# A two-layer graph network on one core: two of the last batch's twelve attention units by TensorE's sums and ScalarE's functions, with 18 steps kept for the last change of layers

## The chip, the cores and the metric

The kernel runs on one core of one Trainium2 chip. A core has TensorE (PE; its weight loads are listed apart as PEld), VectorE (DVE), ScalarE (ACT), GpSimd (POOL) and SyncE (SP), which here only issues transfers. The metric is the time of one execution in microseconds of device time. The kernel before took 3831.26 us, the median of three runs from 3830.42 to 3833.37. The profiled execution took 3836.74 us by that clock and its span in the profile is 3835.0 us, so times read from the trace are within 0.2% of the timed ones.

## The reference

The input has 8 batches of 2048 nodes with 256 features, and a symmetric 0/1 matrix `adj`. Two layers follow one another, each with a residual and a normalisation:

```python
# layer 0: chunked attention, softmax within every 256 keys, masked by adj
scores = clip(q k^T / 8, -10, 10);  scores = where(mask == 0, -10, scores)
attn   = softmax(scores, axis=-1)          # within a chunk; chunks are summed
out    = layernorm(attn v Wo^T + bo + x);  x = layernorm(x + out)
# layer 1: graph attention, 4 heads of 64 features
Wh = x @ W;  s_src, s_dst = per-head dot products of Wh with a
e  = s_src[i] + s_dst[j];  e = where(e > 0, e, 0.2 * e)
e  = where(adj != 0, e, -inf);  alpha = softmax over j
h  = elu(alpha @ Wh);           x = layernorm(x + h)
```

## The kernel before

**Layer 0** runs in 64 slots a batch (4 query groups of 512 nodes, 2 head pairs, 8 chunks). A slot s holds on TensorE the scores of slot s+1 (L377), then the two products of slot s (L412), one for each head of the pair. VectorE clips and masks the scores out of PSUM (L388), ScalarE takes the exponential in two halves (`exps`, L400) and copies each product out of PSUM (L419, tile `raw`), VectorE inverts the denominators (L427), GpSimd scales and adds (L434, L436).

**Layer 1** works on *units*: 12 units are the 4 heads times three groups of 6, 5 and 5 node blocks (`BANKS`). A unit has 16 tiles, one for each block of 128 neighbours. A tile is made by `make`: VectorE computes `e = max(srow, gd) * et` with one instruction over 768 or 640 columns (L712), where `srow` holds factors of the source nodes broadcast to all partitions, `gd` one factor a partition, and `et` the 0/1 edges. Then `use` multiplies it on TensorE with the features `waug` (L732) into the PSUM tile `pa`, 24 or 20 small matmuls a tile. After 16 tiles `close` yields in four pieces: denominators `dn` on VectorE (L755, L756), `hh` on ScalarE (L760), `ee` and `hp` on ScalarE (L764, L766), and `h` on VectorE (L768). `rest` takes one such piece at a time. Tiles `e` have 4 buffers.

**How they are interleaved.** All engines take their instructions in the order in which the program writes them. While batch b runs layer 0, each slot also takes one `step` of batch b-1's layer 1: 3 tiles (`STEP`), written between the slot's two products. In the last batch the final `LATE` = 14 slots take no step; these 14 steps (42 tiles) are kept and laid between the pieces of the last *change of layers* (L996 to L999), the stretch in which the last query group's projection, normalisations and layer-1 factors are made and in which no slot runs. Its last pieces are `factors`: `most` and `spread` find the maximum and the exponentials, and `rows` writes the source factors to `rowD` in DRAM and has GpSimd scale `waug` by `ed` in four multiplications (L657, L659). Then `Layer1` for the last batch is created, whose constructor issues its first transfers of `et` and `srow`, and a *last stage* runs its 12 units alone, 64 steps of 3 tiles, with the closing normalisations of batches 6 and 7 (`Close`, tables `CLOSING_ALONE` and `ENDING`) between them. After the last tile come the last `close` and the last two groups' normalisation and output.

**PSUM.** Eight banks: `psA` holds two tiles of two banks (scores and others), `psC` one bank for products, `psL` two banks for `pa`, and `psM` one bank, shared by many small users: the feature product `pw` of one node block (L566), half of the output projection `po` (L523), and the helpers of `factors`. A tile of a pool with one buffer can't be written before the readers of the one before it are done. From the second batch on both products of a slot use `psC`, so the second waits for the copy of the first.

In the last 18 slots of the last batch (46 to 63), `psM` is used behind the slot's second product by `pw` in slots 46 to 49, 62 and 63, and by `po` in slots 51 and 52.

Of the kernel before, what the change touches and what calls it, by code (L numbers as in the profile page):

```python
# [8 lines left out]
F32 = mybir.dt.float32  # L9
# [13 lines left out]
def adj_resnorm_kernel(  # L23
# [42 lines left out]
    FIRST = [sum(BANKS[:m]) for m in range(len(BANKS))]  # L66
    TILES = len(UNITS) * NT
    STEP = TILES // SLOTS
    LATE = 14
    WIDE = max(BANKS)  # L70
    JG = 4
    assert TILES == STEP * SLOTS and NT % JG == 0

# [39 lines left out]
    clipD = [tc.dram_tile([P, NT, CH], I8, name=f"clipD{q}") for q in range(NCH)]  # L113
    edgeD = [tc.dram_tile([P, NT, n * P], U8, name=f"edgeD{m}") for m, n in enumerate(BANKS)]
    rowD = tc.dram_tile([B, H, N], F32, name="rowD")
    x1D = tc.dram_tile([B, N, F], F32, name="x1D")
    ctxD = tc.dram_tile([B, N, F], F32, name="ctxD")

# [283 lines left out]
    def product(s, k, alone):  # L402
        q, hp, c = where[s]
        if k == 0:
            raws[s] = small.tile([P, 2, QT, D1], F32, tag="raw", name="raw")

        pool, tag = (psL, "psL") if alone and k else (psC, "psC")
        pc = pool.tile([P, QT, D1], F32, tag=tag, name="pc")
        for i in range(QT):
            for u in range(KT):  # L410
                for z in range(2):
                    nc.tensor.matmul(  # L412
                        pc[z * D : (z + 1) * D, i, :],
                        lhsT=probs[s][u][:, k, i * P + z * D : i * P + (z + 1) * D],
                        rhs=vaug[:, KT * c + u, 2 * hp + k, :],
                        start=(u == 0),
                        stop=(u == KT - 1),
                    )
        nc.scalar.copy(raws[s][:, k], pc)  # L419
# [191 lines left out]
    AFTER_0 = {i: lambda o, i=i: o.values((i + 1,)) for i in range(3)}  # L611
    AFTER = {0: lambda o: o.values((2,)), 1: lambda o: o.values((3,))}

    def factors(b, sd, waug):

# [14 lines left out]
        def spread():  # L632
            pb = psM.tile([P, CH], F32, tag="psM", name="pb")
            nc.tensor.matmul(
                pb[:, :H],
                lhsT=st["most"].to_broadcast([H, P]),
                rhs=identf[:H, :H],
                start=True,
                stop=True,
            )  # L640
            nc.vector.tensor_copy(top, pb[:, :H])
            nc.vector.tensor_add(s, s, topb)
            nc.vector.tensor_scalar(s, s, FAR, None, ALU.min)
            nc.scalar.activation(s, s, AF.Exp, scale=1.0 - SLOPE)
            nc.vector.tensor_sub(d, d, topb)
            nc.vector.tensor_scalar(d, d, -FAR, None, ALU.max)
            nc.scalar.activation(ed, d, AF.Exp)
            nc.scalar.activation(gd, d, AF.Exp, scale=SLOPE - 1.0)

# [16 lines left out]


    class Layer1:
        def __init__(self, b, gd, waug):
            self.b, self.gd, self.waug = b, gd, waug  # L670
            self.made = self.used = 0
            self.rows, self.edge, self.e = {}, {}, {}
            self.tail = []
            self.load_edge(0)
            self.load_edge(1)
            self.load_row(0)

        def load_row(self, n):
            if n < len(UNITS):
                m, h = UNITS[n]  # L680
                srow = small.tile([P, WIDE * P], F32, tag="srow", name="srow")
                i0, w = FIRST[m] * P, BANKS[m] * P
                nc.sync.dma_start(
                    out=srow[:, :w], in_=rowD[self.b, h, i0 : i0 + w].partition_broadcast(P)
                )
                self.rows[n] = srow

        def load_edge(self, k):
            n, jg = k // (NT // JG), k % (NT // JG)
            if n < len(UNITS):  # L690
                m, _ = UNITS[n]
                et = edges.tile([P, JG, WIDE * P], U8, tag="et", name="et")
                w = BANKS[m] * P
                nc.sync.dma_start(
                    out=et[:, :, :w], in_=edgeD[m][:, jg * JG : (jg + 1) * JG, :]
                )
                self.edge[k] = et

        def make(self):

            if self.made == TILES:
                return
            k = self.made
            n, j = k // NT, k % NT
            m, h = UNITS[n]
            if j == NT // 2:
                self.load_row(n + 1)
            if j % JG == 0:
# [11 lines left out]
            self.e[k] = e  # L720
            self.made += 1

        def use(self):
            k = self.used
            n, j = k // NT, k % NT
            m, h = UNITS[n]
            if j == 0:
                self.pa = psL.tile([P, CH], F32, tag="psL", name="pa")
            e = self.e.pop(k)
            for i in range(BANKS[m]):  # L730
                for z in range(2):
# [15 lines left out]
                    self.tail.pop(0)  # L747

        def close(self, u, pa):
            m, h = UNITS[u]  # L750
            n = BANKS[m]
            pav = pa[:, : n * D1].rearrange("p (k d) -> p k d", k=n)

# [20 lines left out]
                op1=ALU.add,  # L774
            )

        def step(self):
            self.rest(1)
            for _ in range(STEP):
                self.make()  # L780
                self.use()

    class Close:

# [41 lines left out]
    for g in range(NCH):  # L826
# [28 lines left out]
        12: [(3, "stats")],  # L855
        13: [(3, "finish")],
    }
    CLOSING_ALONE = {
        -1: [(0, "load"), (1, "load")],
        1: [(0, "add")],  # L860
        2: [(0, "stats"), (1, "add")],
        3: [(1, "stats")],
        4: [(0, "finish"), (2, "load")],
        5: [(1, "finish"), (3, "load")],
        7: [(2, "add")],
        8: [(2, "stats"), (3, "add")],
        9: [(3, "stats")],
        10: [(2, "finish")],
        11: [(3, "finish")],
    }  # L870
    ENDING = {
        25: [(0, "load")],
        28: [(0, "add")],
        29: [(0, "stats")],
        31: [(0, "finish")],
        46: [(1, "load")],
        49: [(1, "add")],
        50: [(1, "stats")],
        52: [(1, "finish")],
        SLOTS - 1: [(2, "load"), (3, "load")],  # L880
        SLOTS: [(2, "add"), (2, "stats"), (3, "add"), (3, "stats"), (2, "finish"), (3, "finish")],
    }
    lower = None
    for b in range(B):
        waug = blocks.tile([P, NT, H, D1], F32, tag="waug", name="waug")
# [15 lines left out]
        for s in range(SLOTS):  # L901
            q, hp, c = where[s]
            i = s % QS
            send()
            if s + 3 < SLOTS:
                load_slab(s + 3)
# [25 lines left out]
                    step(group)  # L932
            elif closing:
                closing.do(s, behind=False)
            product(s, 0, not lower)
            if s + 1 < SLOTS:
                for u in range(KT):
                    exps(s + 1, u)
# [2 lines left out]
                    lower.step()  # L941
            elif masks.left():
                masks.step()
            product(s, 1, not lower)

            if before and i in after:
                after[i](before)
# [9 lines left out]

        send()
        before = group
        gd, fs = factors(b, sd, waug)  # L960
        group = None
        every = tuple(range(QT))

# [29 lines left out]
        else:  # L993
# [2 lines left out]
            order = [begin, lambda: before.values((2, 3)), steps[0], step, ctx, step, steps[1], step]  # L996
            order += [steps[2], step, steps[3], step, steps[4], step, steps[5], step, steps[6], step]
            order += [steps[7], step, steps[8], step, steps[9], step, fs[0], step, fs[1], step, fs[2]]
            order += [step, lambda: lower.rest(4)]  # L999
            assert sum(p is step for p in order) == LATE  # L1000
        for piece in order:
            send()
            piece()
        send()
        lower = Layer1(b, gd, waug)

    closing, ending = Closing(B - 2, CLOSING_ALONE), Closing(B - 1, ENDING)
    closing.do(-1)
    for _ in range(STEP):
        lower.make()  # L1010
    for s in range(SLOTS + 1):
        send()
        if s < SLOTS:
            lower.step()
        else:
            lower.rest(4)
        closing.do(s)
        ending.do(s)
    send()
# [42 lines left out]
```

## Time and profile before

| stage of the trace, us from the start | length | what it is |
|---|---|---|
| to 3474.1 | 3474.1 | seven batches and 46 slots of the last |
| 3474.1 to 3501.2 | 27.1 | slots 46 to 49, with steps of layer 1 and `pw` |
| 3501.2 to 3571.3 | 70.1 | slots 50 to 63, without steps |
| 3571.3 to 3628.0 | 56.7 | last change of layers, with 14 steps |
| 3628.0 to 3817.2 | 189.2 | last stage, 192 tiles alone |
| 3817.2 to 3835.0 | 17.8 | last close, two normalisations, output |

The page gives the busy share of each engine (PE 96%, DVE 84%, ACT 51%, POOL 36%) and the span in 40 slices of 96 us. The timeline lists instructions in order of time; repeated ones are merged with their count, and the bracket gives the idle time of the engine before it and what ended that. "x60" matmuls at L732 are three tiles of 640 columns. The trace lacks a few per cent of the matmul records, so that counts of matmuls are not exact.

### The profile page before, as it was taken

What the parts mean: (1) busy time and instruction counts of PE and PEld (TensorE: products, weight loads), DVE (VectorE), ACT (ScalarE), POOL (GpSimd) and SP (SyncE); (2) the same over time, 40 slices, a digit from 0 to 9 for tenths busy, and PEclk for the clock granted to TensorE, in tenths of its full rate; (3) what the DMA queues carried; (4) which work ended last, traced back from release to release, by engine and by line L of the source; (5) the groups of instructions that cost most, each with busy time, mean ns of one, the idle gap of its engine ahead of it and who ended that gap; (6) DMA issues with size and microseconds to landing.
All of it is one profiled execution on the core that took longest, in us unless ns stands there. A gap on an engine that the chain in (4) does not pass through costs nothing. (4 is left out here: it accounts for less than half of the span.)

```text
span 3835.0 us, 160246 instructions
## 1 busy us (share of the span) xinstructions
PE 3696.8 (96%) x72100; PEld 2752.3 (72%) x72100; DVE 3203.6 (84%) x4810; ACT 1950.1 (51%) x3601; POOL 1385.1 (36%) x1202
## 2 busy tenths in 40 slices
PE   9999999999999999999999999999999999999787
PEld 5656677776777777776777767777677777776676
DVE  5876499986999789995999959998699978998798
ACT  4666345555555555554555545555455555555321
POOL 1445233333433343343433324333343434334310
PEclk9999999999999999999999999999999999999999
DMA  6652333333333433333433334333333433333354
GB/s 161 151 113 65 77 101 99 96 87 112 105 95 102 91 117 101 97 101 87 131 99 92 98 92 134 97 95 88 110 110 94 104 86 118 104 99 86 93 149 123
DMA packets 756545, 398.50 MB, mean 104 GB/s; under 512 B 425744, under 2 KB 721040, under 8 KB 755856
## 3 DMA queue, kind: packets, MB, share of 16 engines
q1 hardware_dynamic: 705856, 354.54, 36.3%
q10 hardware_dynamic: 50000, 33.70, 2.7%
q8 instruction: 564, 9.24, 1.0%
q14 instruction: 125, 1.02, 0.1%
HBM read 331.22 MB, written 56.89 MB: 101 GB/s over the span
## 5 line engine op out<-in xcount | busy, mean ns | idle before, releaser
L388 DVE SCALAR_TENSOR_TENSOR pr<-ps,slab 128x1024 f32<-128x1024 f32 x1024 | 1192.5, 1205 | 215.7 <-PE ps L377 211.4
L712 DVE SCALAR_TENSOR_TENSOR e<-srow,gd,et 128x640 f32<-128x640 f32 (+1 forms) x1536 | 1349.1, 934 | 11.2 <-DMA srow<-rowD 5.7
L412 PEld LDWEIGHTS pc<-vaug,pr 128*64 128x64 f32 x32768 | 1040.6, 138 | 442.7 <-issue 253.7
L412 PE MATMUL pc<-vaug,pr 128*64 128x65 f32 x32768 | 1158.4, 224 | 40.9 <-ACT raw L419 32.0
L400 ACT ACTIVATE pr<-pr 128x1024 f32<-128x1024 f32 x1024 | 1050.4, 1057 | 158.1 <-DVE pr L388 143.6
L732 PE MATMUL pa<-waug,e 128*64 128x65 f32 x32768 | 1083.2, 224 | 41.1 <-DVE e L712 39.6
L732 PEld LDWEIGHTS pa<-waug,e 128*64 128x64 f32 x32768 | 1020.8, 139 | 67.7 <-DVE e L712 39.2
L377 PE MATMUL ps<-qT,kT 64*128 64x512 f32 x4096 | 1029.0, 619 | 3.6 <-DVE pr L388 2.6
L434 POOL TENSOR_TENSOR part<-raw,rd 128x512 f32<-128x512 f32 x448 | 467.9, 1044 | 1462.9 <-DVE rd L427 1450.4
L419 ACT COPY raw<-pc 128x260 f32<-128x260 f32 x1024 | 384.9, 377 | 1181.6 <-PE pc L412 1159.0
L377 PEld LDWEIGHTS ps<-qT,kT 64*128 64x128 f32 x4096 | 350.9, 186 | 330.7 <-issue 205.1
L436 POOL TENSOR_TENSOR acc<-acc,part 128x512 f32<-128x512 f32 x448 | 574.2, 1282 | 35.2
L427 DVE RECIPROCAL rd<-raw 128x8 f32<-128x8 f32 x512 | 100.9, 197 | 117.0 <-ACT raw L419 113.2
L434 POOL TENSOR_TENSOR acc<-raw,rd 128x512 f32<-128x512 f32 x64 | 66.8, 1043 | 336.9 <-DVE rd L427 336.1
L760 ACT ACTIVATE hh<-pa,dn 128x64 f32<-128x64 f32 x512 | 114.6, 320 | 100.6 <-DVE dn L756 96.8
L571 PE MATMUL pw<-w_sb,x1T 128*128 128x264 f32 x512 | 142.4, 415 | 8.6 <-DVE x1T L283 8.0
L487 POOL TENSOR_TENSOR rs_c<-rs_c,nhalf 128x4 f32<-128x4 f32 x32 | 55.6, 1737 | 228.4 <-DVE off_c L486 228.4
L321 PE MATMUL pp<-xT,wk_sb 128*128 128x512 f32 x256 | 119.0, 608 | 7.9 <-ACT qT L329 6.6
L527 PE MATMUL po<-wo_sb,qT 128*128 128x256 f32 x512 | 125.0, 389 | 1.1 <-DVE qT L454 0.8
L321 PE MATMUL pp<-xT,wq_sb 128*128 128x512 f32 x256 | 116.2, 596 | 0.0
L337 PE MATMUL pv<-wv_sb,xT 128*128 128x256 f32 x512 | 115.9, 379 | 0.0
L571 PEld LDWEIGHTS pw<-w_sb,x1T 128*128 128x128 f32 x512 | 93.5, 195 | 30.5 <-DVE x1T L283 8.7
(93 smaller groups left out, 1854.8 us busy)
## 6 DMA issues: line engine op xcount, KB each, us to landing
et<-edgeD SPq DMA_DIRECT2D x256, 320.0 KB, 3.1
slab<-clipD SPq DMA_DIRECT2D x512, 128.0 KB, 3.5
et<-edgeD SPq DMA_DIRECT2D x128, 384.0 KB, 3.5
srow<-rowD SPq DMA_DIRECT2D x64, 320.0 KB, 4.4
xg<-in_x_dram SPq DMA_DIRECT2D x32, 512.0 KB, 4.7
x1D<-y ACTq DMA_DIRECT2D x32, 512.0 KB, 3.0
x1g<-x1D SPq DMA_DIRECT2D x32, 512.0 KB, 5.6
out_dram<-o SPq DMA_DIRECT2D x32, 512.0 KB, 3.9
```

Of the source, the lines that this page charges most:

```text
L321: nc.tensor.matmul(pps[c], lhsT=w[:, kc, c * P : (c + 1) * P], rhs=st["xT"][:, kc, :], start=(kc == 0), stop=(kc == KC - 1),)
L377: nc.tensor.matmul(ps[:, k, :], lhsT=kT[rows, hp, t * P : (t + 1) * P], rhs=qT[rows, hp, cols], start=True, stop=True,)
L388: nc.vector.scalar_tensor_tensor(pr, pss[u], -CLIP, slab[:, u, :].unsqueeze(1).to_broadcast([P, 2, CH]), op0=ALU.max, op1=ALU.min,)
L400: nc.scalar.activation(pr, pr, AF.Exp, scale=0.125)
L412: nc.tensor.matmul(pc[z * D : (z + 1) * D, i, :], lhsT=probs[s][u][:, k, i * P + z * D : i * P + (z + 1) * D], rhs=vaug[:, KT * c + u, 2 * ...
L419: nc.scalar.copy(raws[s][:, k], pc)
L434: nc.gpsimd.tensor_mul(part, raw[:, :, :, :D], rd.to_broadcast([P, 2, QT, D]))
L436: nc.gpsimd.tensor_add(accv, accv, part)
L527: nc.tensor.matmul(po[:, k, :], lhsT=qT[:, c, t * P : (t + 1) * P], rhs=wo_sb[:, c, :], start=(c == 0), stop=(c == KC - 1),)
L571: nc.tensor.matmul(pw[:, k, : F + 2 * H], lhsT=self.x1T[:, c, u * P : (u + 1) * P], rhs=w1_sb[:, c, :], start=(c == 0), stop=(c == KC - 1),)
L712: nc.vector.scalar_tensor_tensor(e[:, :w], self.rows[n][:, :w], self.gd[:, h, j : j + 1], self.edge[k // JG][:, j % JG, :w], op0=ALU.max, ...
L732: nc.tensor.matmul(self.pa[z * D : (z + 1) * D, i * D1 : (i + 1) * D1], lhsT=e[:, i * P + z * D : i * P + (z + 1) * D], rhs=self.waug[:, j ...
```

## The change

Two of the twelve units of the last batch's layer 1 (8 and 9: heads 0 and 1 of the third group, 640 columns) no longer use VectorE for their tiles. They are made by a new class `Sums`: TensorE adds in PSUM the mask (0 or -32768, by a matmul with the identity) and the source term (three bf16 parts of it in three partitions, by a matmul with ones), ScalarE adds the neighbour's term as a bias and applies the leaky slope (`Prelu`), and then the exponential. The purpose is to move 32 of the last stage's 192 tiles from VectorE to engines with room. The stage then has 32 steps: 5 tiles of the other ten units (`MOST`) and one of the two.

To prepare this, the change of layers takes on four transfers of the edges (`et2`), four conversions on ScalarE into `near` and `far` (which reuse the memory of `kT` and `vaug`), and at its end `rows`: a transpose, six small VectorE instructions, three stores of the bf16 parts to `partD` and one load of them. `LATE` becomes 18, so that slots 46 to 49 lose their steps and 12 more tiles are laid at the end of the change of layers, after `waug` is handed to GpSimd. In slots 46 to 63 of the last batch the second product goes to `psM`, so that it need not wait for the copy of the first. The closing pieces are placed anew in the shorter tables.

```diff
-    LATE = 14
+    LATE = 18
+    NOT = -32768.0
+    SUMS = (8, 9)
...
-        pool, tag = (psL, "psL") if alone and k else (psC, "psC")
+        tag = alone if alone and k else "psC"
+        pool = {"psC": psC, "psL": psL, "psM": psM}[tag]
...
             nc.vector.tensor_scalar(s, s, FAR, None, ALU.min)
+            if kept:
+                nc.vector.tensor_scalar(kept[0], s, (1.0 - SLOPE) * FAR, None, ALU.min)
...
             nc.vector.tensor_scalar(d, d, -FAR, None, ALU.max)
+            if kept:
+                nc.vector.tensor_scalar(kept[1], d, -1.0, None, ALU.mult)
...
+    class Sums(Layer1):
...
+            def load(j):
...
+                    nc.sync.dma_start(out=ets[j], in_=edgeD[self.m][:, j : j + JG, :])
...
+            def turn(j):
...
+                    nc.scalar.activation(dst, ets.pop(j), AF.Copy, bias=NOT, scale=-NOT)
...
+        def rows(self):
+            pt = psM.tile([P, CH], F32, tag="psM", name="pt2")
+            nc.tensor.transpose(pt[: H * NT, :P], self.s.rearrange("p h t -> p (h t)"), identf)
+            left = small.tile([H * NT, P], F32, tag="left", name="left", bufs=1)
+            nc.vector.tensor_copy(left, pt[: H * NT, :P])
+            for k in range(3):
+                part = small.tile([H * NT, P], BF16, tag="part3", name="part3", bufs=3)
+                nc.vector.tensor_copy(part, left)
+                if k < 2:
+                    nc.vector.tensor_sub(left, left, part)
+                nc.sync.dma_start(out=partD[k].rearrange("h (t p) -> (h t) p", p=P), in_=part)
+            i0 = FIRST[self.m] * P
+            self.row = big.tile([3, H, self.w], BF16, tag="qT", name="row3")
+            nc.sync.dma_start(out=self.row, in_=partD[:, :, i0 : i0 + self.w])
...
+        def sums(self):
...
+            for c0 in range(0, self.w, CH):
+                c1 = min(c0 + CH, self.w)
+                nc.tensor.matmul(
+                    ps[:, c0:c1],
+                    lhsT=identb,
+                    rhs=self.mask(j)[:, c0:c1],
...
+                nc.tensor.matmul(
+                    ps[:, c0:c1],
+                    lhsT=self.ones,
+                    rhs=self.row[:, h, c0:c1],
...
+        def make(self):
...
+            nc.scalar.activation(
+                e, self.ps.pop(k)[:, : self.w], AF.Prelu, bias=self.d[:, h, j : j + 1], alpha=SLOPE
+            )
+            nc.scalar.activation(e, e, AF.Exp, bias=self.minus[:, h, j : j + 1])
...
+            alone = "" if b else "psL"
+            if b + 1 == B and s >= SLOTS - LATE:
+                alone = "psM"
...
-            order += [step, lambda: lower.rest(4)]
+            order += [step] * 5 + [lambda: lower.rest(4)]
             assert sum(p is step for p in order) == LATE
+            sums = Sums(b, kept, sd[:, H:, :], waug, SUMS)
+            loads, turns = sums.masks()
+            for k, (piece, turn) in enumerate(zip(loads, turns)):
+                order[6 + 5 * k : 6 + 5 * k] = [piece]
+                order[9 + 5 * k : 9 + 5 * k] = [turn]
+            order.append(sums.rows)
...
-        lower = Layer1(b, gd, waug)
+        lower = Layer1(b, gd, waug) if b + 1 < B else Layer1(b, gd, waug, others)
...
-    for s in range(SLOTS + 1):
+    for _ in range(2):
+        sums.sums()
+        sums.make()
+    for s in range(STEPS + 1):
         send()
-        if s < SLOTS:
-            lower.step()
+        if s < STEPS:
+            if s % 2 == 0:
+                for _ in range(2):
+                    sums.sums()
+                for _ in range(2):
+                    sums.make()
+            lower.step(MOST)
+            lower.rest(1)
+            sums.rest(1)
+            sums.use()
         else:
             lower.rest(4)
+            sums.rest(4)
```

## The prediction

> **What bounds the kernel now.** I read the page's slices first, then busy times by stage for the part that the edits touch (from slot 46 on), then the timeline at each seam. Nothing before slot 46 differs in the two built instruction orders.
>
> By stage (columns: window, length, then busy us of PE, PEld, DVE, ACT, POOL, then the granted clock):
>
> ```profile
> 3474.09:3501.17 27.08, 27.08 (x548) 20.25 (x545) 23.41 (x31) 13.69 (x30) 8.00 (x7) 1.00 0.53 138
> 3501.17:3571.27 70.10, 62.32 (x1026) 41.85 (x1026) 44.38 (x71) 38.65 (x66) 34.65 (x32) 1.00 0.24 59
> 3571.27:3619.94 48.67, 39.84 (x836) 35.12 (x834) 42.56 (x76) 13.15 (x37) 8.01 (x6) 0.93 0.30 79
> 3619.94:3628.01 8.07, 2.80 (x67) 2.12 (x63) 5.01 (x8) 2.34 (x9) 8.04 (x5) 0.82 0.52 159
> 3628.01:3817.17 189.16, 161.43 (x4076) 139.37 (x4076) 188.11 (x292) 35.32 (x105) 16.52 (x13) 0.95 0.50 143
> ```
>
> The reader sees five regimes. Slots 46 to 49 are TensorE's (27.08 of 27.08 us). Slots 50 to 63 are a chain of waits. The change of layers is a chain through all engines. Its end, 3619.94 to 3628.01, is GpSimd's. The last stage is VectorE's (188.1 of 189.2 us), ScalarE being 81% idle. The change aims at the last.
>
> A plain slot without a step, from the timeline:
>
> ```profile
> 3503.09 1.15 PE L412 MATMUL pc<-vaug,pr 128*64 128x65 f32 x32
> 3504.34 0.38 ACT L419 COPY raw<-pc 128x260 f32<-128x260 f32 x1 [2.62 <-PE pc L412]
> 3504.61 2.01 ACT L400 ACTIVATE pr<-pr 128x1024 f32<-128x1024 f32 x2
> 3504.77 1.15 PE L412 MATMUL pc<-vaug,pr 128*64 128x65 f32 x32 [0.53 <-ACT raw L419]
> ```
>
> The second product waits 0.53 us for the first copy. But the second copy stands on ScalarE behind both exponentials: with scores at 3501.17 it starts at 3506.52 and ends 5.72 us into the slot. That matters below.
>
> The seam where the last `waug` is scaled:
>
> ```profile
> 3619.94 4.15 DVE L712 SCALAR_TENSOR_TENSOR e<-srow,gd,et 128x640 f32<-128x640 f32 x3
> 3620.92 8.94 POOL L659 TENSOR_TENSOR waug<-waug,ed 128x1024 f32<-128x1024 f32 x4
> 3627.50 0.58 DVE L768 SCALAR_TENSOR_TENSOR h<-ee,hp 128x320 f32<-128x320 f32 x1 [2.12 <-ACT hp L766]
> 3628.01 2.67 DVE L712 SCALAR_TENSOR_TENSOR e<-srow,gd,et 128x768 f32<-128x768 f32 x1
> ```
>
> Three tiles take 4.15 us where they take 2.46 elsewhere; a tile beside a `waug` multiplication grows to 2.67 us.
>
> [...] a tile is blocked for about 1.8 us, about one multiplication (1.92 in the seven earlier batches, 1.91 to 2.50 here). [...] five bf16 transposes of 128 columns took 0.39 us with their loads[...]. [...] the trace's 1024-element exponential took 1057 ns[...].
>
> **The change part by part.**
>
> *Slots 46 to 63.* Removing a step frees 1.75 us of TensorE (60 matmuls, 3483.76 to 3485.51), moving the second product to the spare bank frees 0.53 to 0.6. In a plain slot (50, 54 to 61: nine) the period falls from 4.68 to about 4.1, -0.58 each, -5.2; ScalarE's four-part normalisations and VectorE's 2.6 us of statistics return about 0.5. But `pw` and `po` use the same bank directly behind the second product, so they now wait for its copy, 5.72 us into the slot, plus 0.08. Slots 46 to 49: 5.80 + 1.09 (`pw` to the next scores) = 6.9 against 6.77 before. What the step frees becomes wait: +0.5 for the four. Slots 51 and 52: 5.80 + 1.93 (`po`) = 7.73 against 6.61, +2.2; in 52 and 53 the second product also waits for VectorE's sum that empties `po` (4.13 us into the slot; product ends at 5.25, against 4.68), +0.55 for 53. Slots 62 and 63: +1.0. Sum: -0.4.
>
> *Change of layers, before GpSimd's multiplications.* The four conversions [...] lie in ScalarE's idle time (13 of 49 us busy), except the fourth, between `finish` and the copy of x1T. ScalarE ends `finish` at 3604.5, so that copy starts at 3606.8 instead of 3605.36; 0.75 us of slack before `pw` at 3607.15 leaves +0.8. Two added VectorE instructions ahead of the exponentials cost 0.3. The four transfers lie behind `et` transfers that are issued 3.5 us or more before their conversion. Sum: +1.1.
>
> *From 3619.94 to the last stage's first tile.* Before: 8.07 us. After: 15 tiles instead of 3 at 0.80 = 12.0 (spacing in the last stage, 7.17 us for 9). VectorE always has a next tile, so each of the four multiplications should block one: 4 x 1.85 = 7.4; two `dn` pieces and one `h` on the way 1.0; last tile to the end of `h` 3.95 as before (3624.09 to 3628.0): 24.3. Then `rows`: six VectorE instructions, 1.0. Then the transfers, all in SyncE's one queue and in this order: the third store (issue 0.4; `rowD` was readable 1.8 us after its issue), `row3` 0.4, two `et` 0.8, `srow` 0.4, and its landing 3.8 to 4.8. As the load of `row3` waits for the stores, `et` and `srow` stand behind it: about 8.2 after `rows`. Sum 33.5, +25.4. GpSimd is done long before, so nothing of its wait is left. `sums` has its rows some 2 us before the first `e`.
>
> *Last stage.* VectorE before: 64 tiles x 0.927 + 128 x 0.797 = 161.3; six `Close` of 3.06 = 18.4; eleven `dn` and `h` pairs of 0.75 = 8.3; 1.7 blocked at its start: 189.7 against 189.16 in the trace. After: 135.8 + 18.4 + 7.5 = 161.7. TensorE: a 640-column tile takes 0.61 us (0.0304 a matmul, from 124 matmuls in 3.77 us of slot 47), a 768-column tile 0.73. The sums are new: two matmuls of 512 and two of 128 columns, [...] at the pace of float32 here (512 columns 0.48, from eight paired scores in 1.92) 1.2 above. I take 0.65. A two-step round then takes TensorE 10 x 0.73 + 1.22 + 1.3 = 9.8 (768) or 8.6 (640), and VectorE 9.75 or 8.45 without closings. They balance, so TensorE adds a little: 164.5. [...] -24.7.
>
> *Tail.* The two kinds of unit now close one after the other behind the last tile: a second `dn`, `hh`, `ee`, `hp`, `h` in series (3.0, as 3818.08 to 3821.1), less the 0.6 by which the first is earlier, plus 0.6 for the last product. +3.0.
>
> **Sum:** -0.4 + 1.1 + 25.4 - 24.7 + 3.0 = +4.4, 3835.7 us.
>
> **The rivals.** *Faster:* the slots pay fully (4 x 2.1 + 14 x 0.53 = -15.8), and the added tiles run beside GpSimd, as two of three did at 3619.94 (block stays at 3.5, -4). Then -15.8 + 1.1 + 21.5 - 24.7 + 3.0 = -14.9: 3816. For it: VectorE is idle for 3 us at that seam. Against: the bank has one buffer, and the copy stands behind the exponentials. *Slower:* the sums run at 1.2 us (switching weights twice a block, partly filled array), TensorE becomes the bound: rounds of 10.9 and 9.7 give 163 us, and most of the closings' 18.4 come on top, 178. +18: 3849. For it: TensorE is at 85% of this stage. [...] A table switch on ScalarE between Prelu and the exponential is not in the built order, which has one load as before.
>
> **How the numbers follow.** Forecast 0.60, with +-7 for the block, the landings and waits not seen; faster rival 0.18; slower rival 0.22. The bound of 0.2% is 7.7 us: 3823.6 to 3838.9. The forecast's case gives 0.05 / 0.38 / 0.17, the faster rival 0.16 / 0.02 / 0, the slower 0 / 0 / 0.22: rounded, faster 0.21, same 0.40, slower 0.39. The range takes in both rivals' centres: 3815 to 3850.
>
> **What would show it.** In the profile after: `pw` and `po` in slots 46 to 52 ended by ACT `raw`; nine plain slots at 4.1 us; `e` tiles of 2.7 us beside L659's successor; about 33 us from the factors to the first 768-column tile, and VectorE waiting there for `srow`; a last stage of 164 us with both engines over 85% busy. Wrong, if slots 46 to 49 are near 5 us, if the sums' blocks take over 0.9 us a tile, or if `et` and `srow` land while `rows` runs.

## The result, and the profile after

The changed kernel took 3849.22 us, the median of four runs (3848.77 to 3856.88), and the kernel before 3830.91 beside it (3830.42 to 3833.37): a ratio of 1.0051, 95% interval 1.0034 to 1.0069. It is 18.3 us slower, where 4.4 were forecast.

At 460 us, in a stretch that the change doesn't touch, the profiled execution after is already 6.6 us ahead of the one before (granted clock 0.98 against 0.97 in the first 440 us). So stages are compared, from slot 46 on: 360.9 us in the profile before, 380.4 after, +19.5.

The stages after (columns as in the table of before: window, length, busy us of PE, PEld, DVE, ACT, POOL, granted clock, DMA share, GB/s):

```profile
3467.41:3494.82 27.41, 20.36 (x308) 13.27 (x304) 13.84 (x17) 12.32 (x25) 8.67 (x8) 1.00 0.41 103
3494.82:3565.81 70.99, 62.38 (x1026) 41.75 (x1026) 44.55 (x70) 40.00 (x66) 34.46 (x32) 0.98 0.21 51
3565.81:3615.76 49.95, 41.14 (x837) 36.56 (x835) 42.47 (x78) 21.06 (x38) 8.51 (x6) 0.90 0.38 109
3615.76:3650.61 34.85, 19.66 (x318) 13.82 (x318) 21.32 (x28) 9.00 (x24) 10.63 (x5) 0.67 0.24 70
3650.61:3828.63 178.02, 161.06 (x4208) 139.96 (x4208) 162.57 (x258) 78.15 (x158) 15.16 (x12) 0.95 0.45 128
```

| stage | before | after | measured | forecast |
|---|---|---|---|---|
| slots 46 to 49 | 27.08 | 27.41 | +0.3 | +0.5 |
| slots 50 to 63 | 70.10 | 70.99 | +0.9 | -0.9 |
| change of layers, to the factors | 48.67 | 49.95 | +1.3 | +1.1 |
| seam, to the first 768-column tile | 8.07 | 34.85 | +26.8 | +25.4 |
| last stage, to the last product | 190.02 | 178.02 | -12.0 | -24.7 |
| from there to the end | 16.97 | 19.17 | +2.2 | +3.0 |

Five of six rows came within 2 us. The last stage gained half of its forecast. VectorE's 162.57 us there are what was expected (161.7). ScalarE's two functions took 0.78 and 0.83 us. TensorE's 161.06 are more than the working had: its rounds of 9.8 and 8.6 us make about 145. The timeline of one sum, four matmuls of one tile and the start of the next:

```profile
3689.47 0.39 PE L863 MATMUL sum<-near,identb 128*128 128x512 bf16 x1
3689.78 0.09 PEld L870 LDWEIGHTS <-ones 3*128 3x128 bf16 x1 [0.23 <-issue]
3689.79 0.39 PE L870 MATMUL sum<-row,ones 3*128 3x512 bf16 x1
3690.10 0.23 PE L863 MATMUL sum<-near,identb 128*128 128x128 bf16 x1
3690.26 0.23 PE L870 MATMUL sum<-row,ones 3*128 3x128 bf16 x1
3690.42 0.39 PE L863 MATMUL sum<-near,identb 128*128 128x512 bf16 x1
```

From start to start a tile takes 3690.42 - 3689.47 = 0.95 us, not 0.65. The matmuls follow each other at 0.32 us for 512 columns and 0.16 for 128, about 0.1 us more than in the run with padded ones below (0.21 and 0.06). A load is about as long, 0.09 us: that of `ones` starts 0.31 us behind the start of the matmul before it and 0.01 us ahead of its own (3689.78, and 3689.79).

The seam, by VectorE's and then the queue's rows:

```profile
3615.76 4.15 DVE L722 SCALAR_TENSOR_TENSOR e<-srow,gd,et 128x640 f32<-128x640 f32 x3
3620.12 11.94 DVE L722 SCALAR_TENSOR_TENSOR e<-srow,gd,et 128x640 f32<-128x640 f32 x9
3632.39 2.46 DVE L722 SCALAR_TENSOR_TENSOR e<-srow,gd,et 128x640 f32<-128x640 f32 x3
3650.61 1.95 DVE L722 SCALAR_TENSOR_TENSOR e<-srow,gd,et 128x768 f32<-128x768 f32 x2 [10.27 <-DMA srow<-rowD]
```

```profile
3639.23 1.80 SPq L849 DMA_DIRECT2D partD<-part  x3
3642.34 0.86 SPq L852 DMA_DIRECT2D row<-partD  x1
3643.26 0.83 SPq L704 DMA_DIRECT2D et<-edgeD  x2
3644.13 0.43 SPq L693 DMA_DIRECT2D srow<-rowD  x1
```

Beside GpSimd's multiplications three tiles take 4.15 us and nine take 11.94, where three free ones take 2.46. At the end VectorE waits 10.27 us for `srow`, whose load stands behind the stores, `row3` and `et`. Its issue ends at 3644.56; the last 6.05 us are its landing.

In the slots the bank clash came as forecast (TensorE's timeline, slots 47 and 51). In slot 62 `x1T` comes late as well (VectorE's row, then TensorE's):

```profile
3480.03 1.16 PE L575 MATMUL pw<-w_sb,x1T 128*128 128x264 f32 x4 [1.76 <-ACT raw L423]
3504.52 2.00 PE L531 MATMUL po<-wo_sb,qT 128*128 128x256 f32 x8 [1.76 <-ACT raw L423]
3558.17 1.25 DVE L286 STREAM_TRANSPOSE x1T<-x1t 128x1024 f32<-128x1024 f32 x1 [0.38 <-DMA x1t<-x1D]
3559.57 2.10 PE L575 MATMUL pw<-w_sb,x1T 128*128 128x264 f32 x4 [2.48 <-DVE rd L431]
```

### The profile page after: what moved, and what is told of

It reads as the page before. It is cut to its first block, busy times and chain, and to the rows that moved or that the text cites. A ratio compares the mean times of both kernels' runs of the same rounds, so it can differ in the third digit from the quotient of the medians.

```text
span 3847.8 us, 160533 instructions
## 1 busy us (share of the span) xinstructions
PE 3700.9 (96%) x72229; PEld 2758.2 (72%) x72229; DVE 3185.6 (83%) x4787; ACT 2007.6 (52%) x3669; POOL 1387.2 (36%) x1202
## 5 line engine op out<-in xcount | busy, mean ns | idle before, releaser
L722 DVE SCALAR_TENSOR_TENSOR e<-srow,gd,et 128x640 f32<-128x640 f32 (+1 forms) x1504 | 1326.8, 937 | 34.6 <-PE pa L745 19.0
L745 PE MATMUL pa<-waug,e 128*64 128x65 f32 x32768 | 1059.5, 224 | 31.2 <-DVE e L722 30.6
```

The source lines that it names most:

```text
L722: nc.vector.scalar_tensor_tensor(e[:, :w], self.rows[n][:, :w], self.gd[:, h, j : j + 1], self.edge[k // JG][:, j % JG, :w], op0=ALU.max, ...
L745: nc.tensor.matmul(self.pa[z * D : (z + 1) * D, i * D1 : (i + 1) * D1], lhsT=e[:, i * P + z * D : i * P + (z + 1) * D], rhs=self.waug[:, j ...
```

## The experiments

All edits are to the changed kernel. Ratios are to the kernel before on the same chip, with 95% intervals; stage lengths are from each run's trace. "Total" counts from slot 46 against before's 360.9 us.

### What the sums cost

**The source term left out** (in two units the output lacks the source's score):

```diff
-                    stop=False,
-                )
-                nc.tensor.matmul(
-                    ps[:, c0:c1],
-                    lhsT=self.ones,
-                    rhs=self.row[:, h, c0:c1],
-                    start=False,
                     stop=True,
                 )
```

> The changed kernel without the matmuls with ones: the source term is left out of the two units, so two of the four sum matmuls of a tile go. My theory: TensorE bounds the last stage since a tile's four sums take 0.96 us (0.65 in the prediction); without half of them, 0.48 a tile x 32 = 15 us of TensorE go, rounds of two steps fall from 10.2 and 9.1 to VectorE's 9.5 and 8.4, and the stage from 176 to about 165: 10 to 12 us faster. Rival: the stage is long because VectorE and TensorE wait for each other in turn around the closings, whatever the sums cost: at most 4 us faster.

Measured: 3839.07 us, ratio 1.0022 (1.0012 to 1.0031); last stage 167.6, total +8.7. Four matmuls, two tiles, with one matrix:

```profile
3741.40 0.72 PE L863 MATMUL sum<-near,identb 128*128 128x512 bf16 x4
3742.05 2.67 PE L745 MATMUL pa<-waug,e 128*64 128x65 f32 x84
```

They take 0.65 us from start to start. So half of a sum costs 0.33 us with one matrix, the change to the product behind it included, but 0.48 as half of the alternating sequence. It doesn't tell whether any change of matrix is paid or this one.

**Ones padded to 128 rows with zeros:**

```diff
-            self.ones = small.tile([3, P], BF16, tag="ones", name="ones", bufs=1)
-            nc.vector.memset(self.ones, 1.0)
+            self.ones = small.tile([P, P], BF16, tag="ones", name="ones", bufs=1)
+            nc.vector.memset(self.ones, 0.0)
+            nc.vector.memset(self.ones[:3], 1.0)
...
-            self.row = big.tile([3, H, self.w], BF16, tag="qT", name="row3")
-            nc.sync.dma_start(out=self.row, in_=partD[:, :, i0 : i0 + self.w])
+            self.row = big.tile([P, H, self.w], BF16, tag="qT", name="row3")
+            nc.gpsimd.memset(self.row, 0.0)
+            nc.sync.dma_start(out=self.row[:3], in_=partD[:, :, i0 : i0 + self.w])
```

> The same sums, but the source term's matrix of ones and its row are padded from 3 to 128 rows with zeros, so both matmuls of a sum use all rows of the array. In the changed kernel one tile's four matmuls take 0.955 us; with one and the same stationary matrix in all of them (the run without the source term) two tiles' four matmuls took 0.65, so about 0.105 us per matmul is lost where the matrix alternates. Theory A, any change of the stationary matrix is paid: 0.95 us a tile again, last stage 178 us, no change against the changed kernel. Theory B, only a change between 128 and 3 rows is paid [...]: 0.65 us a tile, last stage about 168 us (32 tiles x 0.3), -10 us.

Measured: 3843.38 us, ratio 1.0032 (1.0019 to 1.0044). The same four matmuls with one load of `ones` and the product behind them, and the stage:

```profile
3744.89 0.10 PEld L872 LDWEIGHTS <-ones 128*128 128x128 bf16 x1
3744.89 0.38 PE L865 MATMUL sum<-near,identb 128*128 128x512 bf16 x1
3745.10 0.38 PE L872 MATMUL sum<-row,ones 128*128 128x512 bf16 x1
3745.32 0.22 PE L865 MATMUL sum<-near,identb 128*128 128x128 bf16 x1
3745.37 0.22 PE L872 MATMUL sum<-row,ones 128*128 128x128 bf16 x1
3745.52 0.45 PE L745 MATMUL pa<-waug,e 128*64 128x65 f32 x8
```

```profile
3652.23:3823.22 170.99, 150.59 (x4194) 138.32 (x4208) 162.27 (x258) 78.17 (x158) 14.65 (x12) 0.95 0.48 136
```

The matrices alternate as before, but the load of `ones` starts 0.21 us ahead of its matmul (3744.89, and 3745.10), and 512 columns now take 0.21 us and 128 take 0.06: 0.54 a tile. So theory B: not each change of matrix is paid, but one between 3 and 128 rows is (0.95 - 0.54 = 0.41 us for a tile's four matmuls). Nor is that the only one: from the last sum to the float32 product behind it, with a stationary matrix of 128x64, 0.15 us pass instead of 0.06. TensorE's busy time falls by 10.5 us, the stage by 7.0 (10 had been expected).

**Four identities, then four rows, for two tiles at once:**

```diff
+            for k in ks:
+                for c0, c1 in cs:
+                    nc.tensor.matmul(
+                        self.ps[k][:, c0:c1],
+                        lhsT=identb,
+                        rhs=self.mask(k % NT)[:, c0:c1],
...
+            for k in ks:
+                _, h = self.units[k // NT]
+                for c0, c1 in cs:
+                    nc.tensor.matmul(
+                        self.ps[k][:, c0:c1],
+                        lhsT=self.ones,
+                        rhs=self.row[:, h, c0:c1],
...
```

> The same sums in another order: the four identity matmuls of two tiles first, then their four with ones, so two changes of the stationary matrix for two tiles instead of eight. Theories A and B (a change of matrix is paid): 1.3 + 2 x 0.1 = 1.5 us for two tiles instead of 1.91, 32 tiles make -6.5 us in the last stage. Theory C (the row term is slow by itself, with 3 rows, whatever stands before it): 1.9 us for two tiles as in the changed kernel, no gain.

Measured: 3844.32 us, ratio 1.0037 (1.0024 to 1.005); last stage 173.0 (5.0 less, where 6.5 had been expected).

```profile
3743.76 0.72 PE L863 MATMUL sum<-near,identb 128*128 128x512 bf16 x4
3744.41 0.71 PE L873 MATMUL sum<-row,ones 3*128 3x512 bf16 x4
3745.05 1.15 PE L745 MATMUL pa<-waug,e 128*64 128x65 f32 x32
```

Two tiles take 3745.05 - 3743.76 = 1.29 us instead of 1.91 (theories A and B had 1.5). The 3-row matmuls are as quick as the others (0.64 against 0.65): theory C falls. The price is in the change between the two sizes (1.91 - 1.29 = 0.62 us for six changes fewer).

### What is left of the last stage

Padded ones leave 171.0 us where about 165 were forecast. In the changed kernel, where closings follow each other on VectorE, TensorE shows this:

```profile
3694.51 4.64 PE L745 MATMUL pa<-waug,e 128*64 128x65 f32 x140 [0.81 <-DVE e L722]
3702.62 3.78 PE L745 MATMUL pa<-waug,e 128*64 128x65 f32 x68 [3.47 <-DVE e L722]
3706.33 0.39 PE L863 MATMUL sum<-near,identb 128*128 128x512 bf16 x1
```

After an idle gap of 3.47 us, 68 matmuls take 3.78 us, 0.056 each at a granted clock of 0.54, where 140 before it took 0.033 each at 1.00. The closings cost twice: the gap, and a slow stretch behind it.

**Closings spread, one piece a step,** with padded ones. The last batch's own closings were spread likewise; the second run takes its second group one step later than the first:

```diff
-        1: [(0, "add"), (0, "stats")],
-        2: [(1, "add"), (1, "stats"), (0, "finish")],
-        3: [(1, "finish"), (2, "load")],
+        1: [(0, "add")],
+        2: [(0, "stats")],
+        3: [(0, "finish"), (1, "add")],
+        4: [(1, "stats"), (2, "load")],
+        5: [(1, "finish")],
...
```

In these two runs, and in the two of the fastest version with the same table, the second-last batch's second group is closed so late that the last batch's first unit has overwritten a part of its sums; the instructions are the same, but the output of that group is not.

> The changed kernel with the ones padded to 128 rows and, new, the closings' additions and statistics of the last stage one piece a step (1.2 or 1.9 us of VectorE) instead of up to 3.1 us a step in neighbouring steps. Theory A, the open 6.5 us of the last stage are TensorE's idle gaps at the closings and the half clock behind them: TensorE's waits for VectorE's tiles fall from 19.4 us to below 8, no gap over 2 us, granted clock 0.97 or more, last stage 165 to 167 us instead of 171.0. Theory B, VectorE is simply the bound (162.3 us busy) and the gaps are its surplus in another place: last stage 170 to 171 us whatever the gaps.

> Padded ones and closings spread over the steps, the second group's closing one step later than in d_spread. The other run's first tile to last product was about 169 us with waits still at the closings of the first rounds (two-step rounds of 16.0, 13.3 and 13.0 us instead of 16.6, 11.9 and 15.5 with padded ones alone). Theory A (gaps and the half clock behind them): 165 to 167 us. Theory B (VectorE's own work is the bound): 168 to 171 us. After the earlier run B is the likelier: about 168.5 us, and 3839 to 3842 where before is 3832.

Measured: 3840.80 us (ratio 1.0019, 1.001 to 1.0029) and 3838.83 (1.002, 1.0012 to 1.0028). The last stage took 166.3 and 165.9 us (by this window the first is not the 169 of the second's expectation). The second one's stage and waits (us in total, times, longest):

```profile
3649.44:3815.29 165.85, 149.06 (x4208) 135.48 (x4208) 161.22 (x258) 78.75 (x159) 14.01 (x12) 0.98 0.50 142
```

```profile
PE pa L745 <- DVE e L722: 17.6, 15, 2.4
DVE e L722 <- PE pa L745: 0.5, 2, 0.2
```

TensorE waits as long as before (17.6 against 19.4 us), but in 15 gaps of at most 2.4 us instead of 9 of up to 3.6; the clock is 0.98 instead of 0.95, and VectorE waits for TensorE 0.5 us instead of 4.4. The sum of waits, expected below 8, was a miss; the length, 165 to 167, was a hit for theory A.

How long a gap is doesn't alone decide whether a slow stretch follows. The first of these runs, the second, and the run below in which only GpSimd's place in the program moves:

```profile
3675.39 3.47 PE L745 MATMUL pa<-waug,e 128*64 128x65 f32 x68 [1.94 <-DVE e L722]
3683.40 2.43 PE L745 MATMUL pa<-waug,e 128*64 128x65 f32 x68 [2.41 <-DVE e L722]
3677.37 2.43 PE L749 MATMUL pa<-waug,e 128*64 128x65 f32 x68 [3.20 <-DVE e L726]
```

The same 68 matmuls took 3.47 us behind a gap of 1.94 us, and 2.43 us behind gaps of 2.41 and 3.20.

**The same, the second-last batch's first two groups closed by step 3:**

```diff
...
+        2: [(0, "finish"), (1, "add")],
+        3: [(1, "stats"), (1, "finish"), (2, "load")],
...
```

> Padded ones, and the closings one piece a step, the second-last batch's first two groups closed by step 3 as in the changed kernel. Theory A (the gaps of TensorE at the closings and the half clock behind them): last stage 165 to 167 us. Theory B (VectorE's work of 162 us is the bound, and it waits as often elsewhere): 168 to 171 us, against 171.0 with padded ones alone. The two earlier runs with spread closings were 7.4 us behind before in time, 3 us better than padded ones alone, which speaks for something between: about 168 us.

Measured: 3848.34 us, ratio 1.0036 (1.0022 to 1.005); last stage 172.9.

```profile
PE pa L745 <- DVE e L722: 22.8, 16, 6.2
DVE h L781 <- ACT hp L779: 7.1, 4, 5.6
```

The clock is 0.97, but a new wait is there: `finish` now stands on ScalarE directly behind its statistics and ahead of `hp` of the first unit's close, so VectorE's `h` waits 5.6 us and TensorE 6.2. Without it the stage would be about 167 (an estimate: 172.9 less 5.6). So the 4.9 us of the spread are shown only with the order that loses a part of a group's sums; this order keeps them, and gained nothing against 171.0.

### What the slots and the seam cost

**14 steps kept instead of 18** (the spare bank then serves slots 50 to 63):

```diff
-    LATE = 18
+    LATE = 14
...
-            order += [step] * 5 + [lambda: lower.rest(4)]
+            order += [step] * 1 + [lambda: lower.rest(4)]
```

> The changed kernel with LATE = 14: slots 46 to 49 keep their steps, and one step instead of five is laid behind the factors. My theory: moving the four steps gained nothing in the slots (they became a wait for the spare bank) and cost their full length at the seam, tiles and GpSimd's blocks. Then slots 46 to 49 take 27.1 us (27.4 in the changed kernel), and the stretch from the factors to the last stage's first tile shrinks from 34.9 by 12 tiles x 0.8 and two to three blocks of 1.8, to about 21: in all 13 to 15 us faster than the changed kernel, about 3835. Rival: the four steps do save 2 us each in the slots and lie free at the seam: then this kernel is 4 to 8 us slower than the changed one. Second rival: tiles cost but GpSimd's blocks don't: 9 to 10 us faster.

Measured: 3843.39 us, ratio 1.0032 (1.0021 to 1.0042). Slots 46 to 49 with their steps and without the spare bank:

```profile
3472.32:3499.41 27.09, 27.09 (x549) 20.26 (x545) 23.43 (x31) 13.70 (x30) 8.02 (x7) 1.00 0.54 137
```

27.09 us, against 27.41 after: the four steps had no price there, for the bank's wait took their place. The seam falls by 12.4 to 22.5 us. In this profile 5.3 of that are lost again in the last stage (183.3, clock 0.90 instead of 0.95), total +11.2. In the median it is 6 us faster than the changed kernel, where 13 to 15 had been expected.

**No spare bank:**

```diff
-                alone = "psM"
+                alone = ""
```

> The changed kernel with both products in psC again in all slots of the last batch (LATE stays 18). My theory: the spare bank loses more behind pw and po than it wins in plain slots. Slots 46 to 49 then take 4.68 + 1.09 = 5.8 us each, 23.1 in all instead of 27.4, and slots 50 to 63 go back to 70.1 from 71.0: 5 us faster than the changed kernel. Rival: the bank is a gain of 0.53 a slot: 9 us slower.

Measured: 3848.47 us, ratio 1.0046 (1.0033 to 1.006). Slots 46 to 49:

```profile
3468.31:3491.59 23.28, 21.02 (x308) 13.57 (x304) 13.64 (x16) 12.32 (x25) 7.99 (x7) 1.00 0.40 117
```

4.1 us less, as the clash says. From slot 50 to the start of slot 62 it takes 60.4 us instead of 58.2, and from there to the factors 60.6 instead of 62.7: in these two executions what the bank saves is lost from slot 62 on (with the bank `pw` waits 2.48 us there). The balance is rough, as other runs with the bank took 61.1 to 64.1 us from there to the factors. Nothing is left in the median; the profiled execution, the slowest of this kernel, also had a clock of 0.87 in the last stage (186.9 us).

**Rows ahead of the last five steps:**

```diff
-            order += [step] * 5 + [lambda: lower.rest(4)]
+            order += [lambda: sums.rows()] + [step] * 5 + [lambda: lower.rest(4)]
...
-            order.append(sums.rows)
```

> The changed kernel with sums.rows (transpose, bf16 parts, three stores, one load) directly behind the last piece of factors, ahead of the five steps, so that et and srow of the last stage don't stand behind it. My theory: the 10.3 us in which VectorE waits for srow go, the first 768-column tile follows h at once: 9 to 11 us faster than the changed kernel, the seam 24 to 26 us instead of 34.9. Rival: srow is late for another reason (the load itself, traffic of the steps' et, the x1g loads): under 4 us faster.

Measured: 3846.23 us, ratio 1.0045 (1.0033 to 1.0058). The seam took 24.4 us, -10.4 as expected, but the last stage 189.0, so that the median fell by 3 us and not by 9 to 11:

```profile
3644.24:3833.28 189.04, 173.07 (x4216) 148.36 (x4215) 163.75 (x259) 82.20 (x163) 15.16 (x12) 0.87 0.43 120
3701.41 3.95 PE L745 MATMUL pa<-waug,e 128*64 128x65 f32 x68 [3.46 <-DVE e L722]
3705.29 0.61 PE L863 MATMUL sum<-near,identb 128*128 128x512 bf16 x1
```

The first line is the window, the others the timeline behind the same gap. The sums after it are still slow (0.61 us), where they were at 0.39 in the changed kernel. By the spacing of the matmuls the slow stretch lasts from 3701.4 to about 3713.6, 12 us, against 4 in the changed kernel. The runs of this kernel spread from 3843.8 to 3854.3, and the profiled one is the slowest.

**GpSimd's scaling later.** Its place in the program moved behind the rows:

```diff
+            if not kept:
+                scale()
+
+        def scale():
             nc.gpsimd.tensor_copy(waug[:, :, :, D], ed.rearrange("p h t -> p t h"))
...
-        return gd, [most, spread, rows]
+        return gd, [most, spread, rows, scale]
...
             order.append(sums.rows)
+            order.append(fs[3])
```

> GpSimd's four multiplications that scale the last waug (and its copy) moved from the head of the seam to behind the rows, where VectorE waits for transfers. If each multiplication blocks one of VectorE's tiles, the stretch from the factors to the first 768-column tile falls from 34.9 to about 28 us (four blocks of 1.85 less, 4.15 and 11.94 us for 3 and 9 tiles become 2.4 and 7.25). Rival: the blocks only move to VectorE's row work and the first 768-column tiles, then -2 us or less.

Measured: nothing moved. GpSimd began 0.2 us behind the factors as before, and the seam took 34.85 us: no input of its instructions had come later. Its median, 3858.25 us (ratio 1.0068, 1.0056 to 1.0081), is 9 us above the changed kernel's, with 2 us more in the stages of its profiled execution; that is not explained. Made to wait for a copy of the factors that VectorE makes behind the rows:

```diff
+            edc = small.tile([P, H, NT], F32, tag="edc", name="edc", bufs=1)
+            nc.vector.tensor_copy(edc, ed)
+            scale(edc)
```

> GpSimd's scaling of the last waug made to wait for a 128x64 copy of the factors that VectorE makes behind the rows, so it really runs later (in the run before, with its place in the program alone moved, it still began at once). If each multiplication blocks one of VectorE's tiles, the 3 and 9 tiles of the seam take 2.4 and 7.3 us instead of 4.15 and 11.94, and the stretch from the factors to the first 768-column tile falls from 34.9 to about 28.5 us. GpSimd then works while VectorE waits for the transfers; TensorE's first product of the last stage may wait for the last multiplication, so -4 to -6 by stage. Rival: the blocks are not GpSimd's and the tiles stay at 1.3 us each, 34.9 us.

Measured: 3846.02 us, ratio 1.0039 (1.0027 to 1.0052). VectorE's tiles at the seam:

```profile
3618.55 2.47 DVE L731 SCALAR_TENSOR_TENSOR e<-srow,gd,et 128x640 f32<-128x640 f32 x3
3621.23 7.22 DVE L731 SCALAR_TENSOR_TENSOR e<-srow,gd,et 128x640 f32<-128x640 f32 x9
```

The seam is 28.1 us: the blocks are GpSimd's, 6.4 us of tiles (4.15 + 11.94 against 2.47 + 7.22) and 6.7 of seam.

**The next stage's loads ahead of `row3`'s** (which becomes a piece of its own, `load_rows`):

```diff
...
             order.append(sums.rows)
+            order.append(lambda: built.append(Layer1(b, gd, waug, others)))
+            order.append(sums.load_rows)
```

> The loads of the next stage's first et tiles and first source row are put ahead of the load of row3 in SyncE's queue; nothing else. The prediction said that et and srow stand behind row3, which waits for the three stores. Then srow is issued 2 to 3 us earlier and the first 768-column tile starts at 31.5 to 32.5 us instead of 34.9 (-2 to -3). Rival: srow's own landing sets it, or the sums' row, which now comes later, holds TensorE back by as much: no gain in total.

Measured: the seam falls to 31.0 us (-3.9), so for 3.9 of the 10.3 us the queue's order was in the way; but 3858.76 us, ratio 1.0065 (1.0052 to 1.0077), with 187.0 us in the last stage at a clock of 0.89.

### All together

**Three edits:** 14 steps, rows ahead of the last step, the bank in nine slots only:

```diff
-    LATE = 18
+    LATE = 14
...
+            if b + 1 == B and s >= SLOTS - 14 and i in (2, 6, 7, 8, 9, 10, 11, 12, 13):
                 alone = "psM"
...
+            order += [lambda: sums.rows(), step, lambda: lower.rest(4)]
```

> Three edits at once: 14 steps kept as before instead of 18, the rows and their transfers ahead of the last step, and the spare bank only in slots 50 and 54 to 61, where neither pw nor po uses it. By stage against the kernel before: slots 46 to 49 0, slots 50 to 63 about -5 (nine slots x 0.6), change of layers +2, seam +2.5 instead of +26.8, last stage -4 to -12 (by the granted clock), tail +2.8: -10 to -2 us, 3822 to 3830 where before is 3832. If the granted clock falls to 0.82 in the first half of the last stage as in the two earlier runs with a shorter seam, the upper end holds.

Measured: 3835.83 us, ratio 1.0015 (1.0006 to 1.0023), slower than expected: the seam took 20.6 us (6.8 of them for `srow` behind `row3`), the last stage 186.1 at 0.89.

**And padded ones, rows behind `spread`, the loads ahead; with and without the bank:**

> All that the runs so far point to: 14 steps kept as before, rows directly behind the exponents' arguments, the next stage's loads ahead of row3's, the ones padded to 128 rows, and the spare bank only in slots 50 and 54 to 61. By stage against the kernel before: slots 46 to 49 0, slots 50 to 62 -5.5, change of layers +4, seam +2, last stage 168 instead of 190, tail +2.8: about -18 us, 3812 where before is 3831; if the granted clock falls at the head of the last stage as in other runs with a short seam, 3815 to 3822, less than the 8 us that it cost where TensorE was the bound.

> The same without the spare bank in any slot. Slots 50 to 62 take 60.4 us instead of 54.9, and the change of layers 61.5 instead of 63.5, because slot 62 no longer runs ahead of the transfer of x1t: +2 to +4 us against the version with the bank. Rival: all that the bank saves is waited for at slot 62, no difference.

Measured: 3822.84 us (ratio 0.9977, 0.9967 to 0.9986) and 3826.64 (0.9983, 0.9975 to 0.999). By stage the bank saves 5.5 us from slot 50 to the start of slot 62 and gives 3.0 back behind it: 2.5, as expected. The last stage takes 173.1 and 171.2; the seam is 15.7, not 10, because the rows now run beside GpSimd (VectorE's timeline):

```profile
3617.45 1.89 DVE L851 TENSOR_TENSOR left<-left,part 64x128 f32<-64x128 f32 x1
3619.38 1.83 DVE L849 CAST part<-left 64x128 bf16<-64x128 f32 x1
```

These take 0.28 and 0.22 us elsewhere.

**And GpSimd behind the rows, closings spread** (by the first two tables, then by the third):

> The fastest version so far with the closings spread and GpSimd's scaling behind a copy of the factors that VectorE makes after the rows, so that the four row instructions that took 1.83 to 1.90 us each take 0.22 to 0.28 again (-6.4 us) and two tiles are blocked instead (+3). Seam 12 us instead of 15.7; last stage 167 instead of 173 by theory A, 171 by theory B. A: 3812 to 3816 where before is 3831; B: 3818 to 3820.

> As d_best, with the second group's closing one step later: 3810 to 3817 where before is 3832, a ratio of about 0.995. Seam 9 us or less (VectorE's first 768-column tile at 3620.8, 5 us after GpSimd's first multiplication at 3615.8, in the earlier run), last stage about 170 us.

> The version to set beside both kernels: 14 steps kept, rows directly behind the exponents' arguments, GpSimd's scaling behind a copy of the factors made after the rows, the next stage's loads ahead of row3's, ones padded to 128 rows, the spare bank in nine slots only, closings spread. 3810 to 3816 where before is 3832, a ratio of about 0.995.

Measured: 3813.09 us (ratio 0.9953, 0.994 to 0.9967), 3811.97 (0.9952, 0.9939 to 0.9964) and, with the third table, 3820.93 (0.9969, 0.9958 to 0.9981), 12.9 us below before but above the 3810 to 3816 expected. The seam is 9.5 us in the third (9.7 and 10.6 in the others), near before's 8.1; its last stage is 175.5 with the 5.6 us wait for `hp`, against 166.9 and 166.4. The third leaves the computation whole and beats both kernels; an order that closes the two groups in time without that wait was not tried.

## Why the prediction was wrong

It named the right stages and, within 2 us, the size of five of six, and failed in the last stage. Of the 15.1 us between +4.4 and +19.5, the last stage holds 12.7.

- **The step that failed** is "I take 0.65" for the sums of a tile. It was the author's estimate, below the 1.2 of float32's pace. The nearest row of the trace was the bf16 transposes, but these have matrices of one size (128x128). Here 128-row and 3-row matrices alternate, and a tile took 0.95 us. The slower rival had named it ("switching weights twice a block, partly filled array") with TensorE as the bound, and gave 178 us for the stage and 3849 in all. Both numbers came true, in part by luck: its own price for a sum, 1.2 us, was too high, and with 0.95 its working gives at most 174 for the stage (an estimate: rounds of 10.4 and 9.2 make 155, and the closings 18.4). Nor was TensorE the only bound, as VectorE was busy as long. With equal sizes the tile costs 0.54 us and the stage 171.0: 7.0 of the 12.7 us are shown to be this.
- "TensorE adds a little: 164.5" took two engines that balance over a round, and put the closings where TensorE has work. But two closings leave TensorE without tiles for 3.5 us, and it is slow behind that. Spreading them brought the stage from 171.0 to 166, 4.9 us more, in the two runs that lose a part of a group's sums; the order that keeps them took 172.9, so this part is shown less firmly. Behind a gap of 3.47 us a matmul took 0.056 us instead of 0.033, but behind 1.94 us it took 0.051 in one run, and behind 3.20 us 0.036 in another. What starts a slow stretch, and how long it lasts, 4 us in one execution and 12 in another, stays open. In the profiled executions of the runs that shortened the seam by one edit the last stage took 179.5 to 189.0 us, at clocks of 0.94 to 0.87, and their medians gained 6 us or less; one lost.
- Slots 46 to 49: 27.41 against 27.6 forecast, for the reason given; the fewer steps there bought nothing. Slots 50 to 63: most plain slots took 3.9 to 4.3 us (4.1 forecast), yet the stage lost 0.9 instead of gaining, because slots 62 and 63 took 3.1 us more than before and not 1.0. `pw` of slot 62 starts 6.55 us into the slot instead of 5.77 (slot 47), as `x1T` was ready only at 3559.42, and takes 2.10 us instead of 1.16; the working lacked both.
- Change of layers: +1.3 against +1.1. Four conversions took 2.34 us each; their length in the forecast was the author's estimate.
- Seam: 34.85 against 33.5. The blocks took 6.4 us (7.4), the rows 1.7 (1.0), and from there to the first tile 10.3 (8.2), as the landing of `srow` took 6.05 (3.8 to 4.8). Blocks were counted for VectorE's tiles alone; in a later run a cast of 128 columns, which has one input, grew from 0.22 to 1.83 us beside GpSimd.
- Tail: +2.2 against +3.0.

On weight loads: one of 3 rows took 0.09 us, one of 128 rows 0.10. In the padded run the load of `ones` started 0.21 us ahead of its matmul, and a tile took 0.54 us; with 3 rows it started 0.01 us ahead, and about 0.1 us was paid at each change. Why it starts so late there, no run shows.

## What to carry to other kernels

Price a new matmul by a row of the trace with the same sequence of stationary matrices, their row counts included; a small matrix between large ones can cost more than one padded with zeros (0.95 against 0.54 us a tile here). When two engines balance on paper, look for lumps of one of them: the other then idles, and TensorE can come back slower (0.056 us a matmul instead of 0.033 behind a gap of 3.47 us). Before work is moved out of a stretch, ask which wait ends last there without it: four steps left slots 46 to 49, a bank's wait took their place (27.41 us without the steps, 27.09 with them), and the steps cost 12 us where they went.

## What was not expected of the hardware

- A bf16 matmul took 0.1 us more at each change between a 128-row and a 3-row stationary matrix (512 columns 0.32 instead of 0.21 us), and nothing measurable between two bf16 matrices of 128x128 (0.54 us for four matmuls, against 0.65 with one matrix and the change to the product behind them). From such a matrix to a float32 one of 128x64, 0.1 us was paid again (0.15 instead of 0.06).
- TensorE took 0.051 us a matmul behind an idle gap of 1.94 us in one run, and 0.036 behind 3.20 us in another.
- The granted clock of the last stage was 0.87 to 0.98 in the profiled executions, and the same work took 11 us longer at 0.87 than at 0.95 (189.0 against 178.0).
- A cast with one input took 1.83 us beside GpSimd, where it takes 0.22 elsewhere; one of GpSimd's multiplications took 1.92 us (median of 32 in the profile before).
